# Self products of 32 instead of 24 blocks in the feed-forward stage of a two-layer graph network

## The chip, the core and the metric

The kernel runs on one core of one Trainium2 chip. The metric is the device time of one execution in microseconds (us); the median of three runs of the kernel before is 6163.95.

A core has five engines that this text names as the profile does: PE multiplies matrices, DVE and ACT work on elements, POOL here issues the gathers, SP issues most of the plain transfers. PEld is the loading of weights into PE. A transfer between the device's main memory and the on-chip memory is a DMA.

## What is computed

There are N = 10000 nodes with 512 features, 160000 edges with source, destination and one of four types. Two layers follow one another, each after a layer norm and a relu, each added to its input. Cut to what matters here:

```python
h = relu(layernorm(x))
# layer 0
h_all = einsum('nd,rdf->nrf', h, rel_W) + rel_b        # four messages per node
agg = segment_sum(h_all[src, edge_type], dst) / max(deg, 1)
y = h @ self_W + self_b + agg                          # h @ self_W is the self product
x1 = layernorm(h + y) * ln1_w + ln1_b
f = gelu(x1 @ W1 + b1) @ W2 + b2
x = x + layernorm(x1 + f) * ln2_w + ln2_b
# layer 1, twice with other weights, on h = relu(layernorm(x))
h = relu(h @ W_self + (segment_sum(h[src], dst) / max(deg, 1)) @ W_neigh + b)
x = x + h
```

## The kernel before

The nodes are cut into 78 blocks of 128 and one of 16. The edges come sorted by destination, so a block's incoming rows can be gathered with indirect DMAs, 128 rows of 512 numbers each (256 KB).

The kernel has four stages.

1. Products. A loop over 39 pairs of blocks normalizes the rows, transposes them and makes the four messages per node (line 774) with a seven-product scheme for a pair of blocks; the messages go to `hall_d`. The self product of the pair is made with the same scheme on half widths (`halves`, line 678, 14 products of 256 columns with the sums on DVE) and is stored to `xs_d`, what the norm left goes to `xr_d`. For the blocks in `late` the self product is skipped: `residual` stores the transposed rows to `hT_d` instead. Beside this loop DVE builds the gather lists, a piece in each half pair.
2. Feed-forward, `aligned` up to its line 1207. A loop over the 79 blocks; one turn is called a slot here, i is its number. In slot i the block's gathered rows are added and normalized, its successor's rows are gathered and summed, and a part of an older group's feed-forward products is done: four slots per group of four blocks, two with `up` (line 1030, half of the 8 products each), two with `down` (line 1041, two blocks each).
3. and 4. Two aggregation layers over the 79 blocks, with gathers from `h1_d` and `h2_d`.

In the feed-forward stage:

- `gather` issues 5 gathers of shared rows and 11 of own rows (`mine`) per block on POOL, one more every fourth block and one more every sixteenth. They go into a ring of row buffers, `RINGS[0]` = 28, which are handed out in order. A gather that gets a buffer waits until its last reader is done.
- `sums` adds the shared rows on PE (line 897) into `pa`, of which there are two; `add` adds the 11 own rows to it on DVE (line 908).
- `fetch` (line 971) loads a late block's transposed rows from `hT_d` on SP into a row buffer of the same ring; `residuals` (line 980), one slot later, makes the product in four matmuls of 512 columns, adds the bias on DVE in place and stores the block to `xs_d`. The buffer is free after this store. `LATE` says how many blocks are fetched for which slot; before, all 24 are done by slot 6, the first eight from a buffer of their own.
- `load_res` fetches two blocks of `xr_d`, in turn into one buffer of its own and the two halves of `wself`, the self weights, which nobody needs after the last late block. `scaled` writes the outcome into it, and SP stores it to `xn_d` (line 1134).
- `rests` keeps the middle norm's result (tile `rest`, 11 buffers) from a block's own slot to the slot after its `down`.
- The last norm's result h1 is written on ACT into a tile of two blocks (line 1083), of which there are two, and stored in one DMA (line 1120).
- `down` and `residuals` share the two PSUM buffers of `psO`.

Each engine runs its instructions in the order of the program. On SP an instruction that waits holds all that stand behind it, and so on POOL. Each fp32 matmul of the source shows as two records in the profile.

```python
LATE = (4, 0, 4, 4, 4, 3, 4, 1)
...
if i + 2 < len(LATE):
    if i:
        fetch(LATE[i + 2])
    ready = arrived[len(arrived) - LATE[i + 2]:]
```

Of the kernel before, what the change touches and what calls it, by code (L numbers as in the profile page):

```python
# [8 lines left out]
F32 = mybir.dt.float32  # L9
# [3 lines left out]
AF = mybir.ActivationFunctionType  # L13
# [3 lines left out]
P = 128  # L17
# [4 lines left out]
def kernel(  # L22
# [33 lines left out]
    nc = tc.nc  # L56
    N, D = x.shape
# [42 lines left out]
    wself = const.tile([P, KC, D], F32, name="wself")  # L100
    bself = const.tile([P, D], F32, name="bself")
    dram = ctx.enter_context(tc.tile_pool(name="dram", bufs=1, space=DRAM))

    LATE_SETS = 12
    late = list(range(full - 2 * LATE_SETS - 2, full - 2))
    hT_d = dram.tile([len(late) * P, D], F32, name="hT_d")
    hall_d = dram.tile([N + P, R * D], F32, name="hall_d")
    xs_d = dram.tile([N, D], F32, name="xs_d")
    xr_d = dram.tile([N, D], F32, name="xr_d")
    x1_d = dram.tile([N, D], F32, name="x1_d")  # L110
    xn_d = dram.tile([N, D], F32, name="xn_d")
    h1_d = dram.tile([N + P, D], F32, name="h1_d")
# [24 lines left out]
    def rows_of(t, g):  # L137

        b, nb, r = g
        return t[b * P:b * P + nb * r, :].rearrange("(c p) d -> p c d", p=r)  # L140

    def wide(pool, row, n, name):

        t = pool.tile([P, n], F32, name=name)
        nc.sync.dma_start(t, bass.AP(tensor=row.tensor, offset=row.offset, ap=[[0, P], [1, n]]))
        return t
# [453 lines left out]
    with ExitStack() as s:  # L600
# [127 lines left out]
        for k in range(KC):  # L728
            at = wself[:, k, k * P:(k + 1) * P]
# [4 lines left out]
        if N % P:  # L734
            r = sets[0][2]
# [76 lines left out]
    def aligned(ctxa):  # L812

        psA = ctxa.enter_context(tc.tile_pool(name="psA", bufs=2, space=PSUM))
        ring = []
        RINGS = (28, 56)
        UPPER = -(1 << 12)
        rest = list(range(full))
        blocks = ([full] if N % P else []) + rest

        def height(b):
            return min(P, N - b * P)
# [88 lines left out]
        with ExitStack() as s:  # L911
            ring.append((s.enter_context(tc.tile_pool(name="gat", bufs=1)), RINGS[0]))
            wp = s.enter_context(tc.tile_pool(name="wp2", bufs=1))
            gp = s.enter_context(tc.tile_pool(name="gp", bufs=1))
# [11 lines left out]
            nodes, xrs = {}, {}  # L926

            def pair(t, b, n, name, bufs):

                return (gp.tile([P, 2, D], F32, name=name, bufs=bufs)[:height(b), :n],  # L930
                        rows_of(t, (b, n, height(b))))
# [8 lines left out]
                    nodes[b + c] = v[:, c, :]  # L940

            def load_res(b, n):
                i = len(taken) % 3
                taken.append(b)
                v, at = pair(xr_d, b, n, "xr", 1)
                if i:
                    v = halves[i - 1][:height(b), :n]
                nc.sync.dma_start(v, at)
                for c in range(n):
                    xrs[b + c] = v[:, c, :]  # L950
                xrs[b, n] = v
# [4 lines left out]
                                  allow_slow_non_contiguous=True)  # L956
                return t

            LATE = (4, 0, 4, 4, 4, 3, 4, 1)
            EARLY = 8  # L960
            assert sum(LATE) == len(late) and sum(LATE[:3]) == EARLY <= FC
            halves = [wself[:, :2], wself[:, 2:]]
            waiting, arrived = list(late), []

            def fetch(n, room=None):

                for k, b in enumerate(waiting[:n]):
                    i = late.index(b)
                    t = row_tile() if room is None else room[:, k, :]
                    queue = nc.sync if room is None else nc.scalar  # L970
                    queue.dma_start(t, hT_d[i * P:(i + 1) * P, :])
                    arrived.append((b, t))
                del waiting[:n]

            def residuals(n):

                for b, t in arrived[:n]:
                    po = psO.tile([P, D], F32, name="po")
                    for k in range(KC):
                        nc.tensor.matmul(po, t[:, k * P:(k + 1) * P], wself[:, k, :],  # L980
                                         start=(k == 0), stop=(k == KC - 1))
                    nc.vector.tensor_tensor(t, po, bself, op=OP.add)
                    nc.sync.dma_start(xs_d[b * P:(b + 1) * P, :], t)
                del arrived[:n]
# [5 lines left out]
            nc.scalar.copy(lanes, lane)  # L990
            first_hot = hots(blocks[0], gp, lanes)
            lnb2 = wide(wp, ln1_b, D, "lnb2")
            b2s = gp.tile([P, 2, D], F32, name="h1", bufs=2)[:, 0, :]
            nc.sync.dma_start(b2s, bass.AP(tensor=b2.tensor, offset=b2.offset,
                                           ap=[[0, P], [1, D]]))
            ln1w = wide(wp, ln1_w, D, "ln1w")
# [3 lines left out]
                              allow_slow_non_contiguous=True)  # L1000
            ln2w = wide(wp, ln2_w, D, "ln2w")
            residuals(LATE[0])
            taken = []

            class Group:


# [27 lines left out]
                def down(self, b):  # L1035
                    c, r = self.bs.index(b), self.r
                    if c % 2 == 0:
                        load_res(b, min(2, len(self.bs) - c))
                    po = psO.tile([P, D], F32, name="po")
                    for f in range(FC):  # L1040
                        nc.tensor.matmul(po[:r], self.hid[:, f, c * r:(c + 1) * r], w2s[:, f, :],  # L1041
                                         start=(f == 0), stop=(f == FC - 1))
                    return b, po
# [49 lines left out]
            rests = {}  # L1093
            fed, third = [], []
            now = Scales()
# [13 lines left out]
            def scaled(got, first):  # L1109

                nonlocal third, now
                if first:
                    b, c, pa = first
                    r = height(b)
                    now.apply(nodes[b][:r], pa[:r], c, r, AF.Identity)
                if third:
                    h1, at = pair(h1_d, third[0][0], len(third), "h1", 2)
                    for k, (b, c) in enumerate(third):
                        now.apply(h1[:, k, :], xrs.pop(b), c, height(b), AF.Relu)
                    nc.sync.dma_start(at, h1)  # L1120
                third = []
                last, now = now, Scales()
                for b, v, c in got:
                    r = height(b)
                    last.affine(xrs[b], v[:r], c, r, ln2w, xrs[b])
                    third.append((b, now.stats(xrs[b], r)))
                if first:
                    b, c, pa = first
                    r = height(b)
                    rests[b] = gp.tile([P, D], F32, name="rest", bufs=11)  # L1130
                    last.affine(rests[b][:r], pa[:r], c, r, ln1w, lnb2[:r])
                if got:
                    b, n = got[0][0], len(got)
                    nc.sync.dma_start(rows_of(xn_d, (b, n, height(b))), xrs.pop((b, n)))
# [27 lines left out]
            i = 0  # L1162
            grp = None
            for bs in plan:
                for b in bs:
                    r = height(b)
# [6 lines left out]
                    ready = []  # L1173
# [4 lines that stand above are left out]
                    if i == 1:  # L1178
# [4 lines left out]
                    v = nodes[b]  # L1183
# [4 lines left out]
                    next(part)  # L1188
                    now.finish()
                    scaled(got, first)  # L1190
                    next(part, None)
                    if i + 1 < len(blocks):
# [8 lines left out]
            while queue or fed or third:  # L1201
                got = second()
                part = products(queue.pop(0) if queue else [], None)
                next(part)
                now.finish()
                scaled(got, None)
                next(part, None)


        ring.append((ctxa.enter_context(tc.tile_pool(name="gat2", bufs=1)), RINGS[1]))  # L1210
        for t in (row, orow, *srow):
            nc.vector.tensor_scalar(t, t, R.bit_length() - 1, None, op0=OP.logical_shift_right)
        for step, (h_d, ws, wn, bs) in enumerate(((h1_d, ws1, wn1, bs1), (h2_d, ws2, wn2, bs2))):
            with ExitStack() as s:
# [49 lines left out]
                for i, b in enumerate(blocks):  # L1264
                    r = height(b)
# [304 lines left out]
    with tc.If(go > 0) as cmp:  # L1570
        with ExitStack() as ctxa:
            with tc.manual_schedule():
                aligned(ctxa)
# [31 lines left out]
```

## Time and profile before

| What | us |
|---|---|
| median of three timed runs | 6163.95 (6160.82 to 6165.61) |
| the profiled execution | 7032.07 |
| its span, first to last instruction | 7030.1 |
| product stage | 0 to about 1207 |
| feed-forward stage, first slots | 1207 to 1442 |
| feed-forward stage, other slots | 1442 to 3155 |
| its last products, without gathers | 3155 to 3227 |
| first layer | 3227 to 5160 |
| second layer | 5160 to 7030 |

The profiled execution is much longer than the timed ones. Durations of instructions come from it, and a time in the timed runs has to be inferred from them.

Engines, busy over the span: PE 82%, PEld 38%, DVE 52%, ACT 26%, POOL 53%. In the timeline each line has a start, a duration, engine, line, operation, output and inputs and the number of instructions; a bracket is idle time of that engine before it and what ended it. In the table of stretches each row has the stretch, its length, the busy time (and instructions) of PE, PEld, DVE, ACT and POOL, the granted clock of PE, the busy share of the DMA engines, and what they moved.

### The profile page before, as it was taken

To read this page: it belongs to the slowest core of one execution; us is meant where nothing else is said; L and a number is where in the kernel's file an instruction comes from. 1 tells how busy PE (TensorE), PEld (TensorE's weight loads), DVE (VectorE), ACT (ScalarE), POOL (GpSimd) and SP (SyncE) were. 2 spreads that over 40 slices of the span, in tenths; PEclk is the share of its full clock that TensorE was granted. 3 is DMA by queue.
4 is the path that set the end of the run, shared out by engine and by line. 5 is a ranking of instruction groups with operands and counts; after the bars stand their busy time and mean duration, and the time that the engine had idled before them with its cause. 6 is when DMAs were issued, how large, how long until landed. Compare 5 with 4: busy or idle time off the path is not lost.

```text
span 7030.1 us, 55146 instructions
## 1 busy us (share of the span) xinstructions
PE 5756.5 (82%) x15103; PEld 2675.2 (38%) x15103; DVE 3683.9 (52%) x7447; ACT 1805.0 (26%) x3594; POOL 3716.9 (53%) x3927
## 2 busy tenths in 40 slices
PE   9999999788988889885777777777757777777778
PEld 4555544343433334332333333333323333333333
DVE  8889995466766667661333333333323343434334
ACT  1046660123222223221222222222212121212122
POOL 0011110566666666643666666666556666666664
PEclk9999999899999999997888888988878888898889
DMA  4333344777777777654666666666657676776764
GB/s 156 115 129 123 131 156 149 238 222 225 225 217 217 223 218 229 210 178 157 202 205 205 203 205 204 209 202 204 185 180 218 209 221 211 217 220 212 220 213 154
DMA packets 503502, 1373.79 MB, mean 195 GB/s; under 512 B 82206, under 2 KB 82206, under 8 KB 503054
## 3 DMA queue, kind: packets, MB, share of 16 engines
q0 software_dynamic: 308768, 1008.91, 47.8%
q1 hardware_dynamic: 192734, 358.11, 14.0%
q10 hardware_dynamic: 1680, 3.15, 0.1%
q8 instruction: 122, 2.00, 0.1%
q14 instruction: 198, 1.62, 0.1%
HBM read 1156.54 MB, written 213.30 MB: 195 GB/s over the span
## 4 chain that ended last, share of the span: by engine, by line
PE 61%; issue 19%; another core or an unknown queue 9%; DVE 5%; ACT 3%; DMA 2%; POOL 2%; SPq 0%; POOLq 0%; DVEq 0%; ACTq 0%
PE pa L897 14%; PE pm L774 13%; PE ph L1030 7%; PE po L1247 7%; PE po L1041 6%; PE po L1276 4%; PE pa L879 4%; DVE pa L908 3%; PE pm L678 2%; POOL rows L844 2%; PE pT L172 2%; PE po L980 1%; DMA rows<-h_d,row 1%; PE pT L1018 0%
## 5 line engine op out<-in xcount | busy, mean ns | idle before, releaser
L908 DVE TENSOR_TENSOR pa<-pa,rows 128x512 f32<-128x512 f32 x2574 | 1799.0, 699 | 2026.4 <-remote 1008.8
L844 POOL DMA_INDIRECT rows<-h_d,row x1716 | 1621.9, 945 | 1006.0 <-issue 381.8
L1247 PE MATMUL po<-wns,mTb 128*128 128x512 f32 (+1 forms) x1264 | 737.9, 738 | 836.5 <-issue 653.0
L897 PE MATMUL pa<-rows,hot 128*128 128x512 f32 (+1 forms) x2358 | 1116.1, 613 | 101.1 <-issue 91.1
L844 POOL DMA_INDIRECT rows<-hall_d,row x858 | 822.1, 958 | 497.0 <-issue 196.8
L844 POOL DMA_INDIRECT rows<-h_d,orow x786 | 743.0, 945 | 413.3 <-issue 222.1
L1247 PEld LDWEIGHTS po<-wns,mTb 128*128 128x128 f32 (+1 forms) x1264 | 290.2, 238 | 1270.5 <-issue 1043.6
L897 PEld LDWEIGHTS pa<-rows,hot 128*128 128x128 f32 (+1 forms) x2358 | 456.1, 194 | 706.6 <-issue 680.9
L1030 PE MATMUL ph<-x1T,w1s 128*128 128x512 f32 (+2 forms) x1344 | 582.5, 585 | 74.1 <-ACT hid L1032 37.1
L1276 PE MATMUL po<-wss,hTb 128*128 128x512 f32 (+1 forms) x1264 | 596.3, 616 | 39.6 <-issue 24.5
L1041 PE MATMUL po<-w2s,hid 128*128 128x512 f32 (+1 forms) x1264 | 581.3, 609 | 47.2 <-issue 45.1
L844 POOL DMA_INDIRECT rows<-hall_d,orow x393 | 373.2, 950 | 393.5 <-PE pm L678 203.4
L173 ACT COPY mTb<-pT 128x512 f32<-128x512 f32 (+1 forms) x158 | 91.8, 581 | 1769.5 <-remote 1381.7
L879 PE MATMUL pa<-wss,ident 128*128 128x512 f32 x936 | 427.5, 593 | 0.0
L1030 PEld LDWEIGHTS ph<-x1T,w1s 128*128 128x128 f32 x1344 | 255.5, 198 | 372.5 <-issue 319.3
L1041 PEld LDWEIGHTS po<-w2s,hid 128*128 128x128 f32 (+1 forms) x1264 | 239.5, 193 | 341.9 <-issue 337.3
L513 POOL DMA_INDIRECT win<-rec_d,at x79 | 81.5, 1031 | 529.0 <-PE pe L538 348.2
L1276 PEld LDWEIGHTS po<-wss,hTb 128*128 128x128 f32 (+1 forms) x1264 | 235.9, 197 | 293.1 <-issue 271.1
L866 ACT ACTIVATE hot<-lane,loc 128x128 f32<-128x128 f32 x1098 | 337.8, 392 | 0.0
L774 PE MATMUL pm<-wrel,hT 128*128 128x512 f32 x624 | 296.5, 597 | 0.0
L774 PE MATMUL pm<-wrel,s 128*128 128x512 f32 x624 | 293.3, 592 | 0.0
L897 PE MATMUL pa<-tail,hot 128*128 128x512 f32 x624 | 293.2, 592 | 0.0
(307 smaller groups left out, 6117.9 us busy)
## 6 DMA issues: line engine op xcount, KB each, us to landing
hall_d<-p SPq DMA_DIRECT2D x156, 256.0 KB
hall_d<-u SPq DMA_DIRECT2D x156, 256.0 KB
hb<-h_d SPq DMA_DIRECT2D x156, 256.0 KB
rows<-h_d,row POOLq DMA_INDIRECT x1716
xg<-in_x_dram SPq DMA_DIRECT2D x39, 512.0 KB
xr_d<-xg SPq DMA_DIRECT2D x39, 512.0 KB
xs<-xs_d SPq DMA_DIRECT2D x39, 512.0 KB
h_d<-h SPq DMA_DIRECT2D x39, 512.0 KB
```

Of the source, the lines that this page charges most:

```text
L172: nc.tensor.transpose(p[:, k, :r], rows[:, k * P:(k + 1) * P], ident[:r, :r])
L678: nc.tensor.matmul(pm, a[:, k, :], w[:, k, :], start=(k == 0), stop=(k == KH - 1))
L774: nc.tensor.matmul(pm, a[:, k, :], w[:, k, :], start=(k == 0), stop=(k == KH - 1))
L844: nc.gpsimd.indirect_dma_start(out=t[:n], out_offset=None, in_=table, in_offset=bass.IndirectOffsetOnAxis(ap=idx, axis=0))
L866: nc.scalar.activation(hot[:, t, :], lane, AF.Abs, bias=loc[:, b, t:t + 1], scale=-1.0)
L879: nc.tensor.matmul(p, ident, w, start=True, stop=True)
L897: nc.tensor.matmul(pa[:r], h, v, start=(i == 0), stop=(i == len(work) - 1))
L908: nc.vector.tensor_tensor(pa[:r], pa[:r], t[:r], op=OP.add)
L1030: nc.tensor.matmul(ph[:, :n], w1s[:, k, f * P:(f + 1) * P], self.xT[:, k, :n], start=(k == 0), stop=(k == KC - 1))
L1041: nc.tensor.matmul(po[:r], self.hid[:, f, c * r:(c + 1) * r], w2s[:, f, :], start=(f == 0), stop=(f == FC - 1))
L1247: nc.tensor.matmul(po[:r], mT[:, k, :r], wns[:, k, :], start=False, stop=(k == KC - 1))
L1276: nc.tensor.matmul(po[:r], hT[:, k, :r], wss[:, k, :], start=(k == 0), stop=False)
```

## The change

`LATE_SETS` goes from 12 to 16, so that `late` holds blocks 44 to 75 in place of 52 to 75. `LATE` gets a tail of eight times (0, 0, 0, 0, 1): one block is fetched in each of slots 10, 15, ... 45, and its product is made one slot later. The self weights are thus needed until slot 46, and `load_res` gets three buffers of its own. The room comes from the ring (27 for 28), from `rest` (10 for 11) and from h1, which is written and stored one block at a time.

```diff
-    LATE_SETS = 12
+    LATE_SETS = 16
...
-        RINGS = (28, 56)
+        RINGS = (27, 56)
...
             def load_res(b, n):
-                i = len(taken) % 3
-                taken.append(b)
-                v, at = pair(xr_d, b, n, "xr", 1)
-                if i:
-                    v = halves[i - 1][:height(b), :n]
+                v, at = pair(xr_d, b, n, "xr", 3)
                 nc.sync.dma_start(v, at)
...
-            LATE = (4, 0, 4, 4, 4, 3, 4, 1)
+            LATE = (4, 0, 4, 4, 4, 3, 4, 1) + (0, 0, 0, 0, 1) * 8
...
-            halves = [wself[:, :2], wself[:, 2:]]
...
-            b2s = gp.tile([P, 2, D], F32, name="h1", bufs=2)[:, 0, :]
+            b2s = gp.tile([P, D], F32, name="h1", bufs=2)
...
                 if third:
-                    h1, at = pair(h1_d, third[0][0], len(third), "h1", 2)
-                    for k, (b, c) in enumerate(third):
-                        now.apply(h1[:, k, :], xrs.pop(b), c, height(b), AF.Relu)
-                    nc.sync.dma_start(at, h1)
+                    for b, c in third:
+                        r = height(b)
+                        h1 = gp.tile([P, D], F32, name="h1", bufs=2)[:r]
+                        now.apply(h1, xrs.pop(b), c, r, AF.Relu)
+                        nc.sync.dma_start(h1_d[b * P:b * P + r, :], h1)
...
-                    rests[b] = gp.tile([P, D], F32, name="rest", bufs=11)
+                    rests[b] = gp.tile([P, D], F32, name="rest", bufs=10)
```

More of the change, by code (lines that the diff above doesn't have):

```diff
@@ L1002, in aligned @@
             residuals(LATE[0])
-            taken = []
             class Group:
```

## The prediction

> **What bounds the kernel now.** I read the table of busy time by stretches first, then the PE timeline in two of the stretches, then the queue of gathers on POOL.
>
> ```profile
> core 0: us, PE busy (x) PEld busy (x) DVE busy (x) ACT busy (x) POOL busy (x), PEclk, DMA share, GB/s
> 0.00:1207.00 1207.00, 1194.79 (x3965) 624.83 (x3965) 1038.59 (x3357) 457.81 (x906) 86.69 (x100) 1.00 0.38 133
> ...
> 1442.00:3155.00 1713.00, 1487.38 (x3558) 670.07 (x3557) 1150.92 (x1894) 473.26 (x768) 1085.34 (x1135) 0.93 0.70 216
> ...
> 3227.00:5160.00 1933.00, 1418.64 (x3488) 631.16 (x3489) 657.07 (x955) 432.93 (x963) 1224.04 (x1295) 0.86 0.66 201
> ```
>
> The first stretch is the product stage, the second the feed-forward stage without its first slots, the third the first aggregation layer. In the product stage PE is busy 99% of the time at full clock. In the others PE has holes and a lower clock.
>
> The pace of the product stage is read from the transposes that open each half pair:
>
> ```profile
> 752.94 0.60 PE L172 MATMUL pT<-ident,hg 128*128 128x128 f32 x4
> ...
> 784.94 0.60 PE L172 MATMUL pT<-ident,hg 128*128 128x128 f32 x4
> ...
> 816.94 0.60 PE L172 MATMUL pT<-ident,hg 128*128 128x128 f32 x4
> ...
> 865.27 0.60 PE L172 MATMUL pT<-ident,hg 128*128 128x128 f32 x4
> ...
> 891.22 0.60 PE L172 MATMUL pT<-ident,hg 128*128 128x128 f32 x4
> ```
>
> A pair with its self product takes 32.00 us (twice, 752.94 to 816.94). The second pair of the late kind takes 25.95 us (865.27 to 891.22). Both carry the same list work on DVE, and PE runs back to back in both, so PE sets both paces.
>
> In the feed-forward stage a slot that isn't disturbed looks so:
>
> ```profile
> 2259.10 0.79 PE L897 MATMUL pa<-upper,hot 128*128 128x512 f32 x1
> ...
> 2278.49 0.79 PE L897 MATMUL pa<-upper,hot 128*128 128x512 f32 x1
> ...
> 2299.56 0.79 PE L897 MATMUL pa<-upper,hot 128*128 128x512 f32 x1
> ...
> 2319.35 4.45 PE L897 MATMUL pa<-rows,hot 128*128 128x512 f32 x10
> ```
>
> From sums to sums: 19.39 us with `up` products, 21.07 with a wait of 1.41 for ACT in it, 19.79 with `down` products. PE's own work is thus 19.6 us a slot. The gather queue stands beside it:
>
> ```profile
> 2233.04 0.95 POOL L844 DMA_INDIRECT rows<-hall_d,row  x1 [0.30 <-issue]
> 2234.29 0.95 POOL L844 DMA_INDIRECT rows<-hall_d,row  x1 [0.30 <-issue]
> 2241.77 0.95 POOL L844 DMA_INDIRECT rows<-hall_d,row  x1 [6.54 <-ACT upper L837]
> 2243.03 0.94 POOL L844 DMA_INDIRECT rows<-hall_d,row  x1 [0.31 <-issue]
> ```
>
> One gather every 1.25 us, when nothing holds it; the 6.54 us is a row buffer that wasn't free. A slot has 16 gathers, a 17th every fourth and an 18th every sixteenth: 16.31 x 1.25 = 20.39 us, more than PE's 19.6.
>
> Which of the two binds? The profiled execution took 7032.07 us (span 7030.1), the timed runs 6163.95 in the median, so 868 us of what the profile shows isn't in the timed runs. The page counts 858 + 393 + 25 gathers from hall_d and 1716 + 786 + 50 from h_d: 3828 x 1.25 = 4785 us. With the 1207 us of the product stage that is 5992, and 172 us are left for the three places where the queue must stand still: before the first layer (114.4 us idle in the profile), before the second (60.1) and after the last gather (59). Even those 233 don't fit. So in the timed runs the queue hardly stops inside a stage, and the holes of the profiled feed-forward stage (PE stalls, with PE at half clock in some) are mostly the profiled execution's own. I read the feed-forward stage of the timed runs as paced by the gather queue at 20.4 us a slot, with PE 0.8 us a slot in hand. This is inferred; no view shows it.
>
> **What the Trainium skill says.** Perfetto Trace Analysis, section What "DMA-bound" means, has the issuing engine's sequencer as a limit of its own, whose window in the profile is descriptor generation and not data movement. The even 1.25 us agrees. Trainium Kernel Development and Optimization, section Key Constraints: DMAs issued from SP, ACT and POOL run on the same 16 engines and interleave; so added plain transfers compete with the gathers. The stretch table has these engines at 0.70, not full. DMA: Bandwidth & Descriptors, section Anatomy of one DMA — SWDGE (gpsimd) path, gives 2.0 us + bytes/436e3: 2.6 us for 256 KB, an estimate for queues that this page's fit doesn't cover exactly; the trace shows no landing time for the loads of hT_d.
>
> **The change part by part.**
>
> Four pairs (blocks 44 to 51) leave the product stage's self product. Each drops from 32.00 to 25.95 us: 4 x 6.05 = **24.2 us less**. DVE drops too (7 adds of 0.417 us and 2 of 0.42 a pair), so it can't take over; late pairs already run PE-paced with the list work beside them. Stores stay equal in bytes, 2 x 256 KB in place of 512.
>
> Eight blocks enter the feed-forward stage. Before, 16 records for two blocks (from 1276.98 on) took 6.87 us, so one block is 3.43 us of PE, plus one DVE add of 0.68 us. On PE: 8 x 3.43 = **27.5 us**, spread as one in five slots. Five slots have 5 x (20.39 - 19.6) = 4.0 us of room, so it fits with 0.5 us over. DVE has 1150.92 busy in 1713, about 16 us a slot, so 0.68 in five slots is hidden; if that cover were gone, 8 x 0.68 = 5.4 us. In `down` slots the residual's output holds one of two psO buffers, and the second `down` waits for the residual's add on DVE, which stands behind eleven adds (8.0 us) and the statistics (0.76 + 0.88): ready about 10.4 us after the sums, needed after 3.43 + 6.87 + 0.43 = 10.7. Four of the eight are in such slots; 0 to 4 x 2 us. I take 4 us for all of this.
>
> Each added block also brings a load of 256 KB on SP into a row buffer of the ring and a store. The gather that gets this buffer 27 places later waits for the store, and the whole POOL queue behind it. Paced by the queue, that gather (the sixth own row of block i+2) is due about 12 us after the last row of block i+1 landed; the residual's add is done about 3 us after that landing (0.73 + 0.76 + 0.88 + 0.68), the store 3 to 5 us later: 4 us in hand. Taken as 0; bound above by the rival below. The bytes, 8 x 512 KB = 4.2 MB, would be 19.4 us at 216 GB/s if the DMA engines were full; they aren't, so 0.
>
> Edits with no cost of their own: 27 for 28 row buffers makes POOL wait for an add one gather (1.25 us) earlier, which bites only when it runs far ahead. Ten for eleven buffers of the middle norm: a block's is taken in its slot and freed eight slots later, two at a time, so nine are live at most. Three xr buffers stay three. h1 goes out as single blocks: 39 more DMA issues on SP of 0.36 us, 14 us over the whole stage on a queue that mostly waits for ACT (292.1 us in 11 waits at the h1 store from 1600 to 2900), and the buffer it reuses was stored in a slot before (13.7 us even in the drain). Between 0 and 14; taken as 0, the last 0.4 aside.
>
> Sum: -24.2 + 4 = -20 us: 7032 - 20 = 7012 for the profiled execution if its stalls stayed equal, which they won't to 20 us. The product stage has no stall in the profile, so the 24.2 carries over whole to the timed runs: 6164 - 20 = **6144 us**.
>
> **The rivals.**
>
> PE paces the feed-forward stage in the timed runs too, as the PE holes would say: the wait of 1.41 us for ACT, if it is real, brings PE to about 20 us a slot, the level of the queue. Then all 27.5 us show: -24.2 + 27.5 = +3, 6167. A half way case, or one in which the 4.2 MB slow the gathers (19.4 us), ends at about 6158. Against: the budget of 172 us.
>
> The borrowed buffers stall the gather queue. For it: POOL's waits in the feed-forward stage, over all from 1207 to 3155, have this line:
>
> ```profile
>   DMA xs_d<-rows: 23.1, 3
> ```
>
> Three gathers waited 7.7 us each for exactly such a store, in the first slots. In the stage's rest nothing in the queue can make up a stall, since 20.39 is above PE's 19.6. It decides from 24.2/8 = 3.0 us a time. At 5 us it is -24.2 + 40 + 4 = +20, **6184**; at 7.7 us +41, 6205. Against: those three stood behind four loads and four stores at once on SP, here it is one.
>
> That the change doesn't do what it says: the blocks do move, eight more products are issued in slots 11, 16, ... 46. I give this nothing.
>
> **How the numbers follow.** Forecast 6136 to 6152 with 0.66. PE-paced or DMA-slowed, 6152 to 6172, 0.21. Stalled queue, above 6172, 0.13. Range 6134 to 6172: the low end is the full 24.2 with nothing lost and some us of slots that were late for other reasons. A measurement of this kernel tells about 0.2%, 12 us, from no change. Faster than 6151.6: the forecast and a little of the second case, 0.70. Within: 0.17. Slower than 6176.3: 0.13.
>
> **What would show it.** In the profile after: the product stage ends near 1183 in place of 1207, with four more pairs at 26 us. The feed-forward stage has eight lone groups of 8 records at the residual line, five slots apart. Right: POOL has no new wait on a store of xs_d beyond 3 us. Wrong: such waits of 5 us or more, eight of them, or a gather queue that waits for PE with no PE stall beside it; then the gain is gone. The profile's own stalls can cover 20 us in its span, so the timed comparison decides.

## The result, and the profile after

The changed kernel takes 6138.41 us in the median (6135.77 to 6138.81, six runs), the kernel before, timed beside it, 6163.98. The ratio is 0.996, with a 95% interval of 0.9949 to 0.997: 25.6 us faster (18 to 31 by the interval), where 20 were forecast (6144).

In some sets of runs every execution of the kernel before takes 7017 to 7088 us instead of 6164 (mean granted clock of PE 0.90 instead of 0.98; the reason was not settled), and the profile that the prediction read is of that length, while the profile after is not.

So the comparison needs a profile of 24 late blocks at the shorter time. The run with only the buffer edits (24 blocks, 6159.15 us, told below) gives it. The file of the kernel after is shorter: its line 975 is line 980 of the kernel before, its 1034 is 1041. First, where the queue of gathers starts. Up to here POOL waits for the last product of the product stage. This is the timeline of POOL, with 24 blocks and then in the kernel after:

```profile
1206.48 0.95 POOL L844 DMA_INDIRECT rows<-hall_d,orow  x1 [203.47 <-PE pm L678]
```

```profile
1182.06 0.94 POOL L844 DMA_INDIRECT rows<-hall_d,orow  x1 [203.38 <-PE pm L678]
```

The product stage is 24.42 us shorter. Four more pairs at the late pace are seen in the kernel after, where the first late pair now begins at 721.2, against 850.0 with 24 blocks (PE timeline, the transposes that open the second half of three late pairs, each line one pair after the one before it):

```profile
736.83 0.60 PE L172 MATMUL pT<-ident,hg 128*128 128x128 f32 x4
...
762.78 0.60 PE L172 MATMUL pT<-ident,hg 128*128 128x128 f32 x4
...
788.74 0.60 PE L172 MATMUL pT<-ident,hg 128*128 128x128 f32 x4
```

25.95 and 25.96 us a pair, as the prediction had it.

An added product in the feed-forward stage of the kernel after (PE timeline, slot 11; the lines left out are the rest of the sums, the products with w1 and the transposes):

```profile
1440.75 0.80 PE L897 MATMUL pa<-upper,hot 128*128 128x512 f32 x1
...
1446.36 3.60 PE L975 MATMUL po<-wself,rows 128*128 128x512 f32 x8
...
1463.56 0.79 PE L897 MATMUL pa<-upper,hot 128*128 128x512 f32 x1
```

The slot takes 22.81 us from sums to sums, an `up` slot without a product 19.39. The product thus costs PE its full 3.42 us on the spot. Yet the queue of gathers takes nearly the same time. This is its last gather of the stage, with 24 blocks and then in the kernel after:

```profile
2837.98 0.95 POOL L844 DMA_INDIRECT rows<-hall_d,row  x1 [0.30 <-DMA rows<-hall_d,row]
```

```profile
2814.87 0.94 POOL L844 DMA_INDIRECT rows<-hall_d,row  x1 [0.30 <-PE pT L1011]
```

From the first gather to the last it is 1631.5 us with 24 blocks and 1632.8 us in the kernel after. The eight products cost the queue 1.3 us.

Why, is seen in the table of stretches of the kernel after (stretch, its length, busy time of PE, PEld, DVE, ACT and POOL, clock, share of the DMA engines, GB/s):

```profile
0.00:1183.00 1183.00, 1172.20 (x3853) 605.40 (x3853) 1022.11 (x3321) 458.23 (x906) 84.05 (x100) 1.00 0.39 136
1183.00:1363.00 180.00, 161.99 (x417) 75.75 (x418) 99.34 (x163) 31.23 (x60) 118.28 (x126) 0.91 0.85 289
1363.00:2265.00 902.00, 900.20 (x2314) 422.91 (x2313) 725.67 (x1196) 298.89 (x485) 684.49 (x715) 1.00 0.83 264
2265.00:2801.00 536.00, 515.08 (x1301) 235.59 (x1300) 414.88 (x687) 169.76 (x274) 406.54 (x425) 0.99 0.82 258
```

From slot 7 to about slot 51 (third line) PE is busy 99.8%, and all the added products lie there. In the rest (fourth line) it has 21 us of holes. So PE doesn't have a bit of room in each slot, which would show as a wait beside each product; it is *behind* the queue, and catches up. The distance can be read from two timelines of the kernel after: the last own gather on POOL of the block of slot 7, and the group of adds that reads it on DVE. (Slot 0 is the block of 16 rows, so slot 7 is that of block 6.)

```profile
1352.92 0.95 POOL L844 DMA_INDIRECT rows<-hall_d,row  x1 [0.30 <-DVE pa L908]
```

```profile
1369.03 8.03 DVE L908 TENSOR_TENSOR pa<-pa,rows 128x512 f32<-128x512 f32 x11 [2.54 <-PE pa L897]
```

The group starts 16.1 us after the issue of its last gather, and the last add 23.4 us after it. In slot 45:

```profile
2136.24 0.94 POOL L844 DMA_INDIRECT rows<-hall_d,row  x1 [0.30 <-DMA rows<-hall_d,row]
```

```profile
2132.84 8.01 DVE L908 TENSOR_TENSOR pa<-pa,rows 128x512 f32<-128x512 f32 x11
```

Now the group starts before the last gather is issued; PE has caught up. A slot of PE without an added product is about 19.4 us, one of the queue 20.6 (last own gather of slot 7 at 1352.92, of slot 77 at 2794.79, 70 slots). With 24 blocks PE catches up earlier: the group starts before its last gather from slot 21 on, in the kernel after from slot 35 on, and PE's first wait for a gather after the first slots comes in slot 28 (1816) instead of slot 52 (2288). These are all of PE's waits with 24 blocks from 1777 to 2822, and then those of the kernel after from 1363 to 2265 (what was waited for, us in total, times, longest):

```profile
PE pa L897 <- DMA rows<-hall_d,orow: 25.4, 16, 3.6
PE po L1034 <- DVE rest L1097: 5.0, 9, 1.0
PE pa L897 <- DVE pa L1178: 4.3, 2, 2.2
PE pa L897 <- ACT upper L837: 0.3, 1, 0.3
```

```profile
PE po L1034 <- DVE rows L977: 1.5, 1, 1.5
PE po L975 <- DVE rest L1097: 0.3, 1, 0.3
```

An added product doesn't fill the hole beside it. It puts off the moment from which PE has to wait.

The queue itself is held only at the start. The kernel after has eight gaps over 0.75 us in it in this stage, all before 1320, among them these (timeline of POOL):

```profile
1262.56 0.94 POOL L844 DMA_INDIRECT rows<-hall_d,orow  x1 [5.43 <-DMA xs_d<-rows]
...
1287.38 0.94 POOL L844 DMA_INDIRECT rows<-hall_d,orow  x1 [4.71 <-DMA xs_d<-rows]
...
1317.64 0.94 POOL L844 DMA_INDIRECT rows<-hall_d,orow  x1 [5.38 <-ACT upper L837]
```

They sum to 21.0 us over the usual 0.30, and with 24 blocks to 21.6, there too with waits for stores of `xs_d` (up to 5.1 us). From 1320 to the last gather no gap of POOL is longer than 0.33 us, so nothing there waits for a store of `xs_d`.

### The profile page after: what moved, and what is told of

Read it like the earlier page. It is cut to its first block, busy times and chain, and to the rows that moved or that the text cites. A ratio compares the mean times of both kernels' runs of the same rounds, so it can differ in the third digit from the quotient of the medians.

```text
span 6133.7 us, 55133 instructions
## 1 busy us (share of the span) xinstructions
PE 5641.4 (92%) x15055; PEld 2562.5 (42%) x15055; DVE 3661.5 (60%) x7419; ACT 1800.1 (29%) x3594; POOL 3717.4 (61%) x3927
## 3 DMA queue, kind: packets, MB, share of 16 engines
q1 hardware_dynamic: 195726, 362.30, 16.1%
## 5 line engine op out<-in xcount | busy, mean ns | idle before, releaser
L897 PE MATMUL pa<-rows,hot 128*128 128x512 f32 (+1 forms) x2358 | 1225.8, 636 | 345.1 <-DMA rows<-h_d,orow 318.2
L897 PEld LDWEIGHTS pa<-rows,hot 128*128 128x128 f32 (+1 forms) x2358 | 404.3, 192 | 1105.6 <-DMA rows<-h_d,orow 827.7
L1241 PE MATMUL po<-wns,mTb 128*128 128x512 f32 (+1 forms) x1264 | 572.6, 596 | 1.3 <-ACT mTb L173 1.3
L1023 PE MATMUL ph<-x1T,w1s 128*128 128x512 f32 (+2 forms) x1344 | 559.6, 570 | 8.4 <-ACT hid L1025 8.4
L1034 PE MATMUL po<-w2s,hid 128*128 128x512 f32 (+1 forms) x1264 | 557.4, 595 | 9.4 <-DVE rest L1097 4.8
L1266 ACT ACTIVATE mb<-pa,rdeg 128x512 f32<-128x512 f32 (+1 forms) x158 | 108.5, 687 | 1137.2 <-DVE pa L908 1133.9
L1241 PEld LDWEIGHTS po<-wns,mTb 128*128 128x128 f32 (+1 forms) x1264 | 240.4, 190 | 307.2 <-issue 271.8
L897 PE MATMUL pa<-tail,hot 128*128 128x512 f32 x624 | 309.1, 613 | 49.2 <-DMA tail<-h_d,srow 39.7
```

The source lines that it names most:

```text
L897: nc.tensor.matmul(pa[:r], h, v, start=(i == 0), stop=(i == len(work) - 1))
L1023: nc.tensor.matmul(ph[:, :n], w1s[:, k, f * P:(f + 1) * P], self.xT[:, k, :n], start=(k == 0), stop=(k == KC - 1))
L1241: nc.tensor.matmul(po[:r], mT[:, k, :r], wns[:, k, :], start=False, stop=(k == KC - 1))
L1266: nc.scalar.activation(m[:r], pa[:r], AF.Copy, scale=rdeg[:r, b:b + 1])
```

## The experiments

**The kernel before, for a profile (e1, e6).** No edit.

> The kernel before, unchanged, for a profile whose execution is as long as the timed ones. Theory Q (the gather queue on POOL paces the feed-forward stage): span about 6160; the queue has a gather every 1.25 us from about slot 6 to its end, some 1618 us from its first gather after the product stage to its last, as in the changed kernel (1182 to 2800), with product stage 24 us longer. Rival P (PE paces it): the stretch from the end of the product stage to the last gather is 27 us shorter than in the changed kernel.

> The kernel before, unchanged, again for a profile. Theory Q (the gather queue paces the feed-forward stage as a whole): product stage 24 us longer than in the changed kernel (1182), then some 1618 us from the first gather to the last, as there. Rival P (PE paces): that stretch is 27 us shorter than in the changed kernel.

Both took the long time (7060.16 and 7054.82 us), so they show the stage at that length only. In them the product stage has its usual length (first gather at 1207.0 and 1206.2), but from the first gather to the last the feed-forward stage takes 1948 and 1926 us in place of 1632.

**Products out, and products for nothing (e3, e4, e5, e7, e8).** Out, in `residuals` (the result then lacks the self product of blocks 68 to 75):

```diff
                 for b, t in arrived[:n]:
+                    if late.index(b) >= 24:
+                        nc.sync.dma_start(xs_d[b * P:(b + 1) * P, :], t)
+                        continue
                     po = psO.tile([P, D], F32, name="po")
```

For nothing, in `products`, with (55, 59, 63, 67, 71, 75) or (14, 19, 23, 30, 34, 39) as `MORE`:

```diff
+                if slot[0] in MORE:
+                    po = psO.tile([P, D], F32, name="po")
+                    for k in range(KC):
+                        nc.tensor.matmul(po, wself[:, k, :P], wself[:, k, :],
+                                         start=(k == 0), stop=(k == KC - 1))
```

> The changed kernel without the products and bias adds of the eight added blocks (their load and store stay, so the self product of blocks 68 to 75 is left out of the result). Takes 27.5 us from PE and 5.4 from DVE in the feed-forward stage. Theory Q: the queue paces, nothing is gained, 6134 to 6139. Rival P: PE paces, 6138 - 27 = 6111. Half way (lead of the queue used up in part of the slots): 6120 to 6133.

> The changed kernel plus six products for nothing (four matmuls of 512 columns each, 3.43 us) on PE in slots 55, 59, ... 75, 20.6 us in all, no DMA, no reader. Theory Q: there PE waits for gathers, about 4 us in every four slots, so one product per four slots fits: 6136 to 6143. Rival P: +20.6, 6159.

> The same six products for nothing, but in slots 14, 19, 23, 30, 34 and 39, beside the eight added. Theory Q with a lead: in these slots PE is back to back and lives on the lead of the queue (23 us at slot 7, 4 us at slot 45, where it is used up). 20.6 us more take the lead away about fifteen slots sooner and then hold the queue: +14 to +20, 6152 to 6159. If the lead isn't what matters and only the sum over the stage counts: as in the late slots, 6136 to 6143.

> The changed kernel without the products and bias adds of the eight added blocks (loads and stores stay; the self product of blocks 68 to 75 is left out of the result), again. Against the changed kernel, theory Q: nothing gained, within 5 us. Rival P: 27 us less. The first try, beside a kernel before of 7043, gave 7003, which is 40 less than before and leaves both open.

> Six products for nothing (20.6 us of PE) in slots 14, 19, 23, 30, 34, 39 of the changed kernel, again. Theory Q with a lead of the queue that is used up by slot 45: +14 to +20 against the changed kernel. If only the sums over the stage count: within 5 us of it.

All five took the long time, so they stand beside a kernel before of that length:

| Run | us | before | ratio (95%) |
|---|---|---|---|
| e3, products out | 7002.69 | 7042.75 | 0.9928 (0.99 to 0.9956) |
| e4, six for nothing late | 7019.11 | 7042.75 | 0.9953 (0.9934 to 0.9972) |
| e5, six for nothing in the middle | 7015.99 | 7042.75 | 0.9966 (0.9948 to 0.9984) |
| e7, products out | 7026.23 | 7050.5 | 0.9963 (0.9949 to 0.9978) |
| e8, six for nothing in the middle | 7025.86 | 7050.5 | 0.9958 (0.9944 to 0.9972) |

e7 and e8 differ by 48 us of PE's work (27.5 out, 20.6 in) and by 0.4 us in time; e3 and e5 differ by the same work, by 13 us in the medians and by 0.0038 (27 us) in the ratios, whose intervals just overlap. So there too most of PE's work in this stage doesn't show in the time, though these runs can't tell some ten us from nothing. All five are 24 to 40 us below the kernel before in the median, of which the product stage is 24. What paces the stage there they don't tell; the queue of gathers alone does not, since it is held beside more than 70 of the 79 blocks (gaps over 0.75 us). The absolute times expected were for the shorter time and are not tested.

The reason that I gave for the six in the middle was wrong as well: "take the lead away sooner" has the sign reversed, since a product delays PE and makes the distance larger. The test that follows from the right sign is e12.

**The buffer edits alone (e10).**

```diff
-    LATE_SETS = 16
+    LATE_SETS = 12
...
-            LATE = (4, 0, 4, 4, 4, 3, 4, 1) + (0, 0, 0, 0, 1) * 8
+            LATE = (4, 0, 4, 4, 4, 3, 4, 1)
```

> 24 blocks stay as before; only the buffer edits are made (27 row buffers, ten of the middle norm, three of xr, h1 block by block). Theory Q: same as before within 5 us, so that the whole gain of the change is the product stage's. Rival: the buffers bring 1 to 14 us of loss (39 more stores on SP, a row buffer fewer), or a gain, since load_res no longer hangs on the self weights.

6159.15 us beside 6162.93: ratio 0.9994 (0.9986 to 1.0002). That is no difference that the measurement can tell; the interval has room for a gain of some 8 us and for hardly any loss. From here to the kernel after the spans differ by 6154.9 - 6133.7 = 21.2 us: 24.4 from the product stage, less 1.3 in the queue and about 2 after its last gather, where what costs them was not traced.

**Products for nothing where PE is furthest behind (e12).** As above, with (7, 8, 9, 10, 11, 12).

> The changed kernel with six products for nothing (20.6 us of PE) one in each of slots 7 to 12, where PE is furthest behind the queue: its trace has the last own gather of a block 23 us ahead of the block's last add at slot 7, about as much as the ring lets the queue run ahead. This corrects the reason given for the six in slots 14 to 39, which had the sign of the lead wrong: a product delays PE, so the lead grows. Theory Q with the ring as its limit: PE has about 1 us a slot, so 6 of the 24 us (20.6 and one added block's 3.4) fit, a little more in what room the ring has left, and the queue is held for the rest and never makes it up: +12 to +17 against 6138. If only sums over the stage count (PE waits for gathers after slot 50 and could give the 20.6 back there): 6136 to 6143. Where before is 7043 to 7050: as without them, about 25 less than before, and nothing is told apart.

6153.22 us, 14.8 over the kernel after; 0.9984 of before (0.9977 to 0.999). From the first gather to the last it is 1650.1 us, 17.3 more than in the kernel after. The queue is now held after slot 6 as well (timeline of POOL):

```profile
1389.62 0.94 POOL L844 DMA_INDIRECT rows<-hall_d,row  x1 [2.14 <-PE pa L897]
...
1435.27 0.94 POOL L844 DMA_INDIRECT rows<-hall_d,row  x1 [3.94 <-PE pa L897]
...
1458.10 1.12 POOL L844 DMA_INDIRECT rows<-hall_d,row  x1 [3.12 <-PE pa L897]
...
1484.34 0.94 POOL L844 DMA_INDIRECT rows<-hall_d,row  x1 [5.94 <-PE pa L897]
```

A gather that is to overwrite a row buffer waits for the sums on PE that read it. In slot 12 the last add now comes 30.3 us after the block's last gather, where it was 21.7. It is the largest distance in this profile. With a further 1.78 at 1565.31 these are 16.9 us, 15.4 over the usual 0.30. PE has holes after slot 50 in this profile as well (514.32 busy from 2284 to 2816), so it could give the time back; the queue can't. The sum over the stage isn't what counts. The place is. (The same six products in later slots were run only at the long time. At the shorter one it is the real products of 32 and 40 blocks that show what later slots cost: 27.5 us of PE for 1.3 and for 3.5 us.)

**40 blocks (e9, e11).**

```diff
-    LATE_SETS = 16
+    LATE_SETS = 20
...
-            LATE = (4, 0, 4, 4, 4, 3, 4, 1) + (0, 0, 0, 0, 1) * 8
+            LATE = (4, 0, 4, 4, 4, 3, 4, 1) + (0, 0, 0, 0, 1) * 8 + (0, 0, 1) * 8
```

> 40 blocks in place of 32: eight more leave the product stage and are made one in every third slot from slot 49 to 70, where PE waits for gathers in the trace of the changed kernel. Theory Q: 4 pairs x 6.05 = 24.2 off the product stage, and 27.5 us of PE against some 32 us that PE has spare there: 20 to 24 less than the changed kernel. Rival P: no gain, within 5 us of it.

> 40 blocks in place of 32, the eight more one in every third slot from 49 to 70, again. Theory Q: product stage 24.2 shorter than in the changed kernel, and 20 to 24 less in all: 6115 to 6119 where before is 6164. Where before is 7043 to 7050 the first try gave 32 less than before, and again 25 to 40 less is expected.

e11: 6111.96 us, ratio 0.9917 (0.9903 to 0.993), 26.4 less than the kernel after and 3 below what was expected; the spans of the two profiles differ by 20.7. The first gather is at 1158.38, 23.7 sooner, and the queue takes 1636.3 us from first to last: 27.5 us more of PE's work cost 3.5. (e9, at the long time: 7018.55 beside 7050.5, 0.9948; the first gather is as early, at 1158.7, but only 32 us are gained against before.) With 40 blocks PE has next to nothing left after slot 6 (stretches of e11):

```profile
1158.00:1318.00 160.00, 139.90 (x366) 65.95 (x364) 88.15 (x146) 26.21 (x51) 101.23 (x107) 0.89 0.85 291
1318.00:2778.00 1460.00, 1454.64 (x3731) 681.93 (x3730) 1156.34 (x1904) 473.73 (x768) 1106.83 (x1156) 1.00 0.83 264
```

**40 blocks, fewer of them in the first slots (e13).** The holds at the start are all but one (1.64 us) of the queue's, so fewer products there should end them.

```diff
-            LATE = (4, 0, 4, 4, 4, 3, 4, 1) + (0, 0, 0, 0, 1) * 8 + (0, 0, 1) * 8
+            LATE = (4, 0, 4, 3, 3, 2, 3, 0) + (0, 0, 1) * 21
```

> 40 blocks, with 11 in place of 16 products in the first five slots after the first eight blocks (3, 3, 2, 3 and none in place of 4, 4, 3, 4 and 1), and 21 one in every third slot up to 69. In the trace with 40 the queue is held 25 us in those first slots, and from slot 6 on PE is busy 99.6%. Theory Q: what the queue gains at the start is lost in part at the end, since PE then has 5 more products after slot 6 and hardly any room: 0 to 20 less than 40 blocks as tried (6112), most likely 10. Rival: PE alone binds from slot 6 on, so nothing is gained or 5 lost.

6102.44 us, ratio 0.9901 (0.9885 to 0.9918): 9.5 less than e11 (9.9 by the spans of the profiles), 36 less than the kernel after, the fastest here. The holds fall from 24.7 us to 7.3, and the last gather comes 16.3 us sooner (2778.38 for 2794.65). About 5 of them are lost before the next layer's first gather, 99.6 us after the last one of this stage in place of 94.5. PE now has no room left (stretches of e13):

```profile
1318.00:2765.00 1447.00, 1447.00 (x3716) 678.66 (x3715) 1148.82 (x1895) 470.92 (x762) 1097.72 (x1146) 1.00 0.83 266
```

PE is busy throughout, and still behind when the stage ends: the last block's last add comes 6.1 us after its last gather, in place of 3.8 in e11. That is 2.3 of the 5 us; the rest was not traced.

## Why the prediction was right

Its direction and its main term were right, and the 20 us that it forecast lie inside the interval of the 25.6 measured. That the sum came this near is in part luck, as the second point shows.

- The product stage: 24.2 forecast, 24.42 measured. From the profile with the buffer edits alone to the kernel after, 21.2 of them arrive.
- The 4 us for what the added blocks cost in the feed-forward stage: about 3 measured (1.3 in the queue, 2 after its last gather), so the size was right, but not the reason. Of the waits of `down` for the residual's add, 0 to 4 of 2 us in the working, one of 1.5 us is there; the 2 us at the end were not thought of. What is left up to 25.6 stands beside the 3.8 us that the buffer edits gained in their own run, which that run can't tell from nothing.
- PE's 27.5 us in the feed-forward stage: each product takes its 3.43 us, and the sum is hidden behind the queue, as forecast. The working "five slots have 4.0 us of room" was the right balance read in the wrong way. There is no room in a slot at that point; PE is behind, and the added products put off the point at which it has caught up. That they fit needs two things which the working did not ask for: the ring must hold what the queue is ahead (e12 shows the price where it doesn't), and PE must catch up before the stage ends.
- The transfers (4.2 MB) at 0: no hold of the queue after 1320, so they cost nothing that shows. The loads of the eight added blocks landed 4.7 to 8.9 us after their issue, where the prediction's estimate for 256 KB was 2.6; the product comes a slot later, and none of PE's waits is for them.
- The buffer edits at 0: confirmed within the interval of e10.
- The gather's pace: 20.39 us a slot forecast from 1.25 us, 20.6 measured over 70 slots. When nothing holds it a gather comes every 1.25 us, but a few take longer, and the mean is 1.26.
- "The holes of the profiled feed-forward stage are mostly the profiled execution's own": this step failed, though its conclusion held. In e1 and e6 (7060.16 and 7054.82 us) the queue is held in the same way, and the timed runs beside them are as long, so such holes don't belong to the profiled execution alone. That the conclusion held was luck. Comparing the span with the timed median rightly showed that the profile was not that of the timed runs it was compared with; the explanation didn't follow from it.
- The rival in which PE paces: refuted by the lengths of the queue with 24, 32 and 40 blocks (1631.5, 1632.8 and 1636.3 us, with 27.5 us more of PE at each step), not by the budget of 172 us, which was too rough to be more than a hint.
- The rival of the borrowed buffers: its waits exist, up to 5.4 us, but in the first slots and equally with 24 blocks. The added fetches cause none. (The 7.7 us "each" of the prediction was the mean of three, of which the longest was 11.7.)

## What to carry to other kernels

When two engines feed each other through a ring, read the distance between them and its course, not the holes slot by slot. Work added to the engine that is behind is nearly free while it can still catch up and the ring isn't full. Where the ring is full it costs most of its price, even if there are holes later: here 14.8 of 20.6 us. Before work is moved into such a stage, find where the slower queue is held; there it may not be added, and from there it should be taken away. And where a profile's span is 14% above the timed median, the holes in it say little about the timed runs.

## What the runs showed of the hardware

- The gathers of 256 KB were issued every 1.25 us when nothing holds them (0.95 busy and 0.30 between). Over the 1142 issued from slot 7 to slot 77 of the kernel after the mean was 1.26 us, with the DMA engines busy 0.82 to 0.83.
- The eight added plain loads of 256 KB landed 4.7 to 8.9 us after their issue, beside these gathers.
- Four fp32 products of 512 columns, eight records in the profile, took PE 3.42 us in slot 11 of the kernel after.
